# Shared layers of two mixtures read the router's transposed rows; results of the second mixture summed six tiles later, last loads issued ahead of the stores

## The chip, the cores and the metric

The kernel runs on one core of a Trainium2 chip. Its engines work side by side: TensorE (PE; weight loads are listed apart as PEld), VectorE (DVE), ScalarE (ACT), GpSimd (POOL), and SyncE (SP), which here only issues transfers. Each engine takes its own instructions in order and waits on semaphores. The metric is the device time of one execution, in microseconds, of the slowest core; here there is only one. The kernel before took 831.38 us (median of three runs, 828.76 to 834.36).

## The reference

The input x is 16 batches of 128 rows of 256 numbers in 32 bits, with a context of the same shape. Four layers are added to x one after the other, each scaled by tanh of a gate and fed with a layer norm of x:

```python
x = x + tanh(g_xattn[0]) * ssm(ctx, ctx, layernorm(x))        # causal convolution of k (x) v with a kernel, times q
x = x + tanh(g_ffn[0])   * ffn0(layernorm(x))
x = x + tanh(g_xattn[1]) * attention(layernorm(x), ctx, ctx)  # causal, 16 heads of 16
x = x + tanh(g_ffn[1])   * ffn1(layernorm(x))

def ffn0(x):   # 8 experts, 2 for each row, and a shared layer of 1024 hidden
    shared = (silu(x @ sw1.T) * (x @ sw2.T)) @ sw3.T
    top = top_k(sigmoid(x @ router_w.T) + expert_bias, 2)
    return shared + sum(weight(top) * expert(x))               # experts: silu(h1) * h2, 128 hidden

def ffn1(x):   # 32 experts, 6 for each row, and a shared layer of 256 hidden
    shared = square(relu(x @ Ws1.T)) @ Ws2.T
    idx, w = top_6_of_the_4_best_groups(sigmoid(x @ Wr.T + br))
    return shared + sum(w * (square(relu(x @ W1.T)) @ W2.T))   # 128 hidden
```

Each mixture ("ffn") thus uses the same normalised rows twice: for its router and experts, and for its shared layer.

## The kernel before

**Tiles.** A batch b is a tile of 128 rows; `xs[b]` holds it in the on-chip memory throughout. `CHUNKS` cuts the 16 batches into (0-3), (4-7), (8-11), (12-13), (14-15) for the first mixture and attention. `GROUPS` does so for the second mixture, with the last two batches apart.

**Turning rows.** A matrix product needs rows transposed, features on the partitions. `turned` (L197) does it: for each tile one VectorE operation normalises (L211), two TensorE transposes write to PSUM (L214), and one ScalarE copy for two tiles (L216) puts it into a tile `xT` of 128 x 2 x up to 512. In both mixtures this runs twice for each tile. Once for the router: the normalised rows go to `row`, which is also what is sent to the experts, and the transposed ones to `xT_f0{c}` or `xT1_{g}` (names tp_f, lg_r for the router's scores). And once more for the shared layer: rows `xn_s`, transposes `tp_s`, copies `xT_s` (first mixture) and `xTs` (second). `stats` keeps mean and reciprocal deviation (mv, rs) for the second time.

**Stage 1, the convolution,** fills the first 110 us. **Stage 2, the first mixture:** `sends0` (L697) normalises, chooses two experts and scatters each row to its place in a DRAM array `sent0` by indirect transfers from POOL (L725). `shared0` (L639) computes the shared layer of a chunk in 8 blocks: pg, pu (L617), silu and product (hs, L432/433), os (L669). `paced` ties the scatters to hs of the block beside them. `tiles0` takes expert tiles of 128 sorted rows back (got, L756), computes two at a time (xt, gu, eo) and stores them to DRAM; `combine0` gathers a row's two results (L812). **Stage 3, attention,** goes batch by batch (sc L858, ex L875, avT L896), and the rest of the first mixture runs between its steps. Transfers of keys and values (L831, L832) stand on SP.

**Stage 4, the second mixture:** `dispatch` (L951) norms, routes and scatters the rows of a group to `sent`, six places each (L978); `shared1` (L922) does the shared layer: p (L617), relu and square on ACT, o_sh (L625), sum on VectorE (L633). These steps lie beside the last batches of attention. Then `tiles1` (L1164) goes over 114 tiles of 128 expert rows, and further ones if there are more rows. One load (got, L1176) brings six tiles and waits for all scatters to `sent`. Two tiles at a time: copy of weights on ACT (wt, L1187), transposes xt and copy (L1190, L1192), eh (L1197), relu on ACT (er), product on VectorE (ehs, L1207), eo (L1209), copy on ACT (ey, L1218). One scatter per tile by POOL (L1234) writes 128 result rows to their places in the DRAM array `parts`.

**Summing.** A row's six results lie side by side in `parts`. `fetch` (L1137) loads two of six for a batch, once the tiles that can hold its rows are through; it waits for scatters up to five before. `add_fetched` (L1144) adds two products to `xs[b]` (L1148) and, after the third of these, stores the batch (L1150). In the kernel before a fetch is issued at each tile, for the third group of batches two, and is added three tiles later or when over two are held. The last four batches, b12 to b15, are summed after all tiles by `sum_last` (L1152): three loads, six scalings on ACT (L1158), one strided reduction on VectorE (L1160), one addition (L1161), the store.

**Order.** The kernel is written as lists of steps, which `woven` (L1030) interleaves. A scheduler then places the instructions on the engines by its own estimates; on each engine that order is fixed when the kernel is built. `follow` and `after` add a dependency. SP issues all ordinary transfers in one queue, in order; an issue whose wait is not met holds those behind it.

Of the kernel before, what the change touches and what calls it, by code (L numbers as in the profile page):

```python
# [33 lines left out]

E0, SH0, TOPK0 = 8, 8, 2
PARTS0 = [(0, 8), (8, 16)]
NT0 = 8 * TOPK0 + E0 - 1
# [6 lines left out]
GRP = 6  # L44
SURE = 114
FEW = 3
W1_ROW = KC * P + D
# [6 lines left out]
def flamingo(ctx: ExitStack, tc: tile.TileContext, a: dict, out: bass.AP):  # L54
# [163 lines left out]
    def columns(xT, n):  # L218
        return lambda j: xT[:, :, 2 * j * P : min(2 * j + 2, n) * P].rearrange("p c (k t) -> p k c t", t=P)
# [158 lines left out]
    def chunk_T(c, label, scale=1.0, norm=None):  # L378
# [4 lines left out]
        return xT  # L383


    def router(xT, n, rw, ne, label):
# [251 lines left out]

    def shared0(c, norm):  # L639

# [5 lines left out]
        def turn():  # L646
            got["xT"] = chunk_T(c, "s0", norm=norm)

# [46 lines left out]

    norms0 = {}

    def sends0(i):
# [6 lines left out]
        def norm(c):  # L705
            n = CHUNKS[c][1] - CHUNKS[c][0]
            tiles = list(range(*CHUNKS[c]))
            rows = [work.tile([P, ROW], F32, tag="row", name=f"row0_{b}", bufs=8) for b in tiles]
            got.setdefault("rows", []).extend(rows)
            got["xT"] = xT = work.tile([P, KC, TOK], F32, tag="xT", name=f"xT_f0{c}", bufs=4)  # L710
            norms0[c] = stats(tiles, f"f0{c}", keep=True)
            turned(work, tiles, *norms0[c], columns(xT, n), f"f0{c}", keep=lambda k: rows[k][:, :D])

# [207 lines left out]

    def shared1(mv, rs, g):  # L922

# [4 lines left out]
        def turn():  # L928
            got["xT"] = xT = work.tile([P, KC, TOK], F32, tag="xT", name=f"xTs_{g}", bufs=4)
            turned(work, list(range(b0, b1)), mv, rs, columns(xT, b1 - b0), f"s1{g}")  # L930

# [19 lines left out]
    def dispatch(g):  # L951
# [5 lines left out]
        def norm():  # L957
            got["rows"] = rows = [
                work.tile([P, ROW], F32, tag="row", name=f"row{b}", bufs=8) for b in range(b0, b1)
            ]  # L960
            got["xT"] = xT = work.tile([P, KC, TOK], F32, tag="xT", name=f"xT1_{g}", bufs=4)
            tiles = list(range(b0, b1))
            got["norm"] = stats(tiles, f"f1{g}", keep=True)
            turned(work, tiles, *got["norm"], columns(xT, n), f"f1{g}", keep=lambda k: rows[k][:, :D])

# [26 lines left out]
        for t in range(n):  # L992
            sends += [lambda t=t: send(t), *wait[1:]]
        shares[g] = lambda: shared1(*got["norm"], g)
        return [norm, *wait[1:], choose, *wait, place, *sends]
# [44 lines left out]
    def sums0(c):  # L1040
        return [lambda b=b: combine0(b) for b in range(*CHUNKS[c])]

    def with_sums0(c):

        steps = shared0(c, norms0[c])
        for k, add in enumerate(sums0(c)):
            steps[3 + k] = lambda now=steps[3 + k], add=add: (now(), add())
        return steps + [nothing, lambda: begin(c), nothing]
# [3 lines left out]
    for step in sendA[:2]:  # L1052
        step()
    woven(shared0(0, norms0[0]), sendA[2:] + [nothing] * 2)
    more = shared0(1, norms0[1])
    woven(tiles0(0, gotA, scatA, "sc"), [nothing] * 3 + sendB + [nothing] * 6, more[:5])
    woven(sums0(0), more[5:8])
    begin(0)
    beside = [
        lambda: more[8:-1] + [lambda: (more[-1](), [step() for step in sums0(1)])] + tiles0(1, gotB, scatB)  # L1060
        + [lambda: begin(1), nothing],
# [58 lines left out]
    def group(b):  # L1120
        return next(c for c, (b0, b1) in enumerate(GROUPS) if b < b1)
# [11 lines left out]

    todo = [(b, k0) for b in range(GROUPS[FEW][0]) for k0 in range(0, TOPK1, 2)]
    fetched = []

# [6 lines left out]

    def add_fetched():  # L1144

        _, b, k0, part = fetched.pop(0)
        for k in range(2):
            V.scalar_tensor_tensor(xs[b], part[:, k, :], gates[:, b, k0 + k : k0 + k + 1], xs[b], ALU.mult, ALU.add)  # L1148
        if k0 + 2 == TOPK1:
            nc.sync.dma_start(out=out[b], in_=xs[b])  # L1150

    def sum_last(b):  # L1152

        part = work.tile([P, TOPK1, D], F32, tag="big", name=f"part{b}", bufs=BIGS)
        for k0 in range(0, TOPK1, 2):
            load_results(part[:, k0 : k0 + 2], b, k0, len(results))
        for k in range(TOPK1):
            S.activation(part[:, k, :], part[:, k, :], AF.Copy, scale=gates[:, b, k : k + 1])  # L1158
        s = work.tile([P, D], F32, tag="xn", name=f"sum{b}", bufs=3)
        V.tensor_reduce(s, part.rearrange("p k d -> p d k"), AX.X, ALU.add)  # L1160
        V.tensor_tensor(xs[b], xs[b], s, ALU.add)  # L1161
        nc.sync.dma_start(out=out[b], in_=xs[b])

    def tiles1(t0, t1):  # L1164
        for t in range(t0, t1):
# [79 lines left out]

            while fetched and (fetched[0][0] <= t - 3 or len(fetched) > 2):
                add_fetched()
            for _ in range(2 if todo and group(todo[0][0]) + 1 == FEW else 1):
                if todo and t + 1 >= last_tile(group(todo[0][0])) + 6:
                    fetch(t)  # L1250
# [11 lines left out]
    with tc.If(used > SURE * P):  # L1262
        tiles1(SURE, NT1)
    for b in range(GROUPS[FEW][0], B):
        sum_last(b)

# [51 lines left out]
```

## Time and profile before

| what | us |
|---|---|
| runs, median (lowest to highest) | 831.38 (828.76 to 834.36) |
| profiled execution | 832.41, its span 830.6 |
| granted TensorE clock, mean | 0.919 |

The profiled execution is the span and 1.8 us around it. Busy time by stretch, in us of TensorE and VectorE, with the granted clock:

| stretch | what runs | length | PE | DVE | clock |
|---|---|---|---|---|---|
| 110 to 180 | shared layer of chunk 0, routing, scatters | 70 | 62.57 | 36.82 | 0.85 |
| 180 to 250 | first expert tiles, shared layer of chunk 1 | 70 | 67.13 | 33.27 | 0.98 |
| 560 to 633 | routing and shared layer of the second mixture | 73 | 60.00 | 51.79 | 0.91 |
| 633 to 718 | expert tiles of the second mixture | 85 | 76.41 | 40.37 | 0.96 |
| 718 to 802 | the same, with fetched results | 84 | 63.20 | 54.72 | 0.93 |
| 802 to 831 | sums of the last four batches | 29 | 0 | 17.56 | |

A row of the list of groups reads: line, engine, operation, names (buffer numbers left out), shapes, count, then busy us and mean ns of one, and what the engine's idle time ahead of these was ended by. In a timeline or the chain, a line begins with the start and the length in us; a bracket gives idle time ahead and what ended it. The chain is followed back from the end of the execution: at each step to what released the instruction. Some rows of groups that the change touches:

```profile
L1148 DVE SCALAR_TENSOR_TENSOR x<-part,gates,x 128x256 f32<-128x256 f32 x72 | 33.9, 483 | 19.1 <-DMA part<-parts 18.1 <-DVEq L1262 0.5
L211 DVE TENSOR_SCALAR xn_s<-x,mv_f,rs_f 128x256 f32<-128x256 f32 x32 | 12.7, 411 | 1.7 <-PE tp_at L214 0.7 <-PE tp_s L214 0.5 <-PE pos L568 0.3
L214 PE MATMUL tp_s<-ident,xn_s 128*128 128x128 f32 x64 | 12.5, 322 | 2.6 <-DVE xn_s L211 1.0 <-ACT xTs L216 0.7 <-ACT pT L885 0.6
L1160 DVE TENSOR_REDUCE sum<-part 128x256 f32<-128x1536 f32 x4 | 11.0, 2762 | 6.5 <-ACT part L1158 6.5
```

### The profile page before, as it was taken

Reading aid. Unit: us, or ns where it says so; the run is one execution under the profiler, and the core shown is the slowest. Engines: PE = TensorE matmul, PEld = TensorE weight load, DVE = VectorE, ACT = ScalarE, POOL = GpSimd, SP = SyncE. Lnnn points to the kernel's source line nnn. Section 1 sums busy time; section 2 is a strip of 40 time slices with the busy share of each in tenths; the row PEclk is TensorE's granted clock in tenths of the full one; section 3 lists DMA queues with packets and bytes.
Section 4 is the critical chain, followed back from the end, with each engine's and each line's share of the span. In section 5 each row is a group of like instructions: output and inputs, shape, how many; then the busy total and the mean of one; then the engine's idle time right before and its main releaser. Section 6 shows DMA issues by size and latency. Waiting matters only on the chain.

```text
span 830.6 us, 12160 instructions
## 1 busy us (share of the span) xinstructions
PE 703.4 (85%) x3928; PEld 496.4 (60%) x3928; DVE 541.2 (65%) x1579; ACT 367.6 (44%) x811; POOL 332.9 (40%) x326
## 2 busy tenths in 40 slices
PE   6999979989999799999969989958867999788820
PEld 3444445567775577656547747735546898677720
DVE  5999995335446754568667874685883555476756
ACT  2110037115322666652356354426524777566624
POOL 3756702300516100012272057007462677766640
PEclk8999978999999999999979987969987999999975
DMA  8999996122442233541143034063125676788575
GB/s 266 327 371 274 269 262 166 58 72 83 154 131 83 64 102 106 132 116 30 46 124 65 13 89 118 15 164 113 67 100 190 210 228 190 247 291 262 187 244 180
DMA packets 134016, 128.97 MB, mean 155 GB/s; under 512 B 42976, under 2 KB 117888, under 8 KB 133824
## 3 DMA queue, kind: packets, MB, share of 16 engines
q1 hardware_dynamic: 120704, 91.61, 39.5%
q0 software_dynamic: 13152, 36.52, 12.3%
q8 instruction: 32, 0.52, 0.3%
q14 instruction: 32, 0.26, 0.1%
q10 hardware_dynamic: 96, 0.05, 0.0%
HBM read 64.23 MB, written 63.92 MB: 154 GB/s over the span
## 4 chain that ended last, share of the span: by engine, by line
PE 46%; DVE 25%; DMA 10%; issue 7%; ACT 6%; POOL 3%; ACTq 1%; SPq 1%; DVEq 0%; POOLq 0%
PE y L339 7%; DMA part<-parts 4%; PE gu L782 4%; PE eo L1209 3%; PE sc L858 3%; PE pu L617 3%; PE pg L617 3%; PE eh L1197 3%; DVE mn L869 3%; PE eo L792 2%; PE pt L882 2%; PE os L669 2%; ACT ex L875 2%; PE avT L896 2%; PE lg_r L391 2%
## 5 line engine op out<-in xcount | busy, mean ns | idle before, releaser
L978 POOL DMA_INDIRECT sent<-row,dst x96 | 94.0, 979 | 123.8 <-DVE dst L609 94.3
L1234 POOL DMA_INDIRECT parts<-ey,to x114 | 111.6, 979 | 58.9 <-issue 23.2
L875 ACT ACTIVATE ex<-sc,mn 128x128 f32<-128x128 f32 x256 | 71.6, 385 | 68.0 <-DVE mn L869 67.9
L812 POOL DMA_INDIRECT part<-parts,places x32 | 31.2, 975 | 144.6 <-DVE rd L912 88.8
L339 PE MATMUL y<-kv,toe 128*128 128x512 f32 x192 | 85.0, 597 | 0.0
L1209 PE MATMUL eo<-wt,ehs 128*128 128x256 f32 x228 | 62.0, 403 | 17.4 <-DVE ehs L1207 17.3
L331 POOL TENSOR_TENSOR kv<-cT 128x1024 f32<-128x1024 f32 x32 | 60.6, 1893 | 38.0 <-PE y L339 33.2
L725 POOL DMA_INDIRECT sent<-row,places x32 | 31.2, 976 | 103.5 <-DVE places L504 38.2
L1187 ACT COPY wt<-wts 128x512 f32 x114 | 66.3, 620 | 13.9 <-issue 8.6
L617 PE MATMUL pg<-xT_s,wts 128*128 128x512 f32 (+1 forms) x160 | 66.3, 535 | 1.9 <-DVE silu L432 1.9
L1197 PE MATMUL eh<-xts,wt 128*128 128x128 f32 x456 | 64.7, 286 | 2.8 <-ACT wt L1187 2.8
L1197 PEld LDWEIGHTS eh<-xts,wt 128*128 128x128 f32 x456 | 62.2, 201 | 8.2 <-ACT wt L1187 4.1
L617 PE MATMUL pu<-xT_s,wts 128*128 128x512 f32 (+1 forms) x160 | 63.7, 517 | 1.9 <-DVE hs L433 1.9
L669 PE MATMUL os<-wts,hs 128*128 128x256 f32 x256 | 65.0, 387 | 0.0
L339 PEld LDWEIGHTS y<-kv,toe 128*128 128x128 f32 x192 | 36.0, 192 | 41.2 <-issue 29.1
L669 PEld LDWEIGHTS os<-wts,hs 128*128 128x128 f32 x256 | 48.4, 194 | 15.7 <-issue 9.7
L1209 PEld LDWEIGHTS eo<-wt,ehs 128*128 128x128 f32 x228 | 40.9, 197 | 25.2 <-DVE ehs L1207 20.7
L1192 DVE COPY xts<-xt 128x512 f32<-128x512 f32 x57 | 38.7, 686 | 25.5 <-PE xt L1190 18.7
L869 DVE TENSOR_REDUCE mn<-sc 128x4 f32<-128x512 f32 x64 | 41.6, 684 | 20.3 <-PE sc L858 20.0
L782 PEld LDWEIGHTS gu<-xts,wt 128*128 128x128 f32 x368 | 46.4, 196 | 8.6 <-DVE xts L776 4.8
L782 PE MATMUL gu<-xts,wt 128*128 128x128 f32 x368 | 49.2, 283 | 1.9 <-DVE xts L776 1.8
L1218 ACT COPY ey<-eo 128x512 f32<-128x512 f32 x57 | 33.4, 586 | 33.7 <-PE eo L1209 29.3
(250 smaller groups left out, 1360.0 us busy)
## 6 DMA issues: line engine op xcount, KB each, us to landing
sent<-keys SPq DMA_DIRECT2D x1, 17018.0 KB
got<-sent SPq DMA_DIRECT2D x19, 804.0 KB, 5.0
part<-parts SPq DMA_DIRECT2D x48, 256.0 KB, 4.7
sent<-keys SPq DMA_DIRECT2D x2, 2944.0 KB
got<-sent SPq DMA_DIRECT2D x22, 256.0 KB, 3.0
parts<-ey SPq DMA_DIRECT2D x22, 256.0 KB, 2.1
wts<-in_sw SPq DMA_DIRECT2D x3, 1024.0 KB, 11.8
wts<-in_w SPq DMA_DIRECT2D x3, 1024.0 KB
```

Source lines behind the costliest of these rows:

```text
L331: G.tensor_tensor(kv, c[:, :, hs].unsqueeze(3).to_broadcast(full), c[:, :, hs].unsqueeze(2).to_broadcast(full), ALU.mult)
L339: T.matmul(y[:, lb * TOK : (lb + 1) * TOK], lhsT=t[:, off : off + P], rhs=kv[:, kc * HALF : (kc + 1) * HALF].rearrange("p b i j -> p (b i ...
L617: T.matmul(ps, lhsT=w(kc), rhs=xT[:, kc, :n], start=(kc == 0), stop=(kc == KC - 1))
L669: T.matmul(o[:, k * D : (k + 1) * D], lhsT=hs[j][:, t * P : (t + 1) * P], rhs=wC[:, j, :], start=False, stop=(j == SH0 - 1 and k == len(ts ...
L782: T.matmul(gu[:, half * D + u * P : half * D + (u + 1) * P], lhsT=wt[:, u, w : w + P], rhs=xt[:, u * D + kc * P : u * D + (kc + 1) * P], s ...
L869: least = V.tensor_reduce(mn[:, 4 * r : 4 * r + 4], scs[r].rearrange("p (h t) -> p h t", t=P), AX.X, ALU.min)
L875: S.activation(ex[:, i, :], scs[r][:, at : at + P], AF.Exp, bias=mn[:, i : i + 1], scale=-1.0)
L978: ins = G.indirect_dma_start(out=sent[:, :], out_offset=bass.IndirectOffsetOnAxis(ap=dst[:, t, k : k + 1], axis=0), in_=row, in_offset=None,)
L1187: S.copy(wt[:, i], wts[:, bass.ds(offsets[u % GRP], W1_ROW)])
L1197: T.matmul(eh[:, i * P : (i + 1) * P], lhsT=wt[:, i, cols], rhs=xt[:, i * D + kc * P : i * D + (kc + 1) * P], start=(kc == 0), stop=(kc == ...
L1209: T.matmul(eo[:, i * D : (i + 1) * D], lhsT=h[:, i * P : (i + 1) * P], rhs=wt[:, i, KC * P :], start=True, stop=True,)
L1234: ins = G.indirect_dma_start(out=parts[:, :], out_offset=bass.IndirectOffsetOnAxis(ap=to[:, t % GRP : t % GRP + 1], axis=0), in_=y[:, t % ...
```

## The change

It has three parts.

*Shared layers.* They no longer normalise and transpose a second time; they take the router's `xT`. For the first two chunks of the first mixture (`HERE = 2`) this is the tile in the on-chip memory itself. For the others, and for all six groups of the second mixture, `put` writes the tile to a DRAM array and `again` reads it back into a new tile before the shared layer. That is 9 stores and 9 loads on SP, of 128, 256 or 512 KB. One block more of chunk 1's shared layer goes ahead of attention's first queries (`more[5:9]`).

*Summing.* For the first two groups of batches a fetch is issued at every second tile instead of every one, up to three may be held, and each is added six tiles later (`LATE`) instead of three. Each addition has a dependency on the copy of the current pair's transposed rows (`turned_rows`). A finished batch is stored when the next one is finished.

*The end.* All loads of the last four batches are issued first. The stores of the batches finished by then, and of the last four, wait for the last load. The strided reduction is replaced by one addition of 128 x 768 and three of 128 x 256.

```diff
--- before.py
+++ after.py
@@ -33,6 +33,7 @@
 WARM = 22
 
 E0, SH0, TOPK0 = 8, 8, 2
+HERE = 2
 PARTS0 = [(0, 8), (8, 16)]
 NT0 = 8 * TOPK0 + E0 - 1
 W0_ROW = 3 * D
@@ -43,6 +44,7 @@
 GROUPS = [(0, 4), (4, 8), (8, 12), (12, 14), (14, 15), (15, 16)]
 GRP = 6
 SURE = 114
+LATE = 6
 FEW = 3
 W1_ROW = KC * P + D
 W1_END = E1 * W1_ROW
@@ -382,6 +384,17 @@
         turned(work, tiles, mv, rs, columns(xT, len(tiles)), f"{label}{c}", scale=scale)
         return xT
 
+    def put(xT, n, label):
+
+        kept = dram.tile([P, KC, n], F32, tag=f"kept_{label}", name=f"kept_{label}")
+        nc.sync.dma_start(out=kept, in_=xT[:, :, :n])
+        return kept
+
+    def again(kept, n, label):
+        xT = work.tile([P, KC, TOK], F32, tag="xT", name=f"xT_{label}", bufs=4)
+        nc.sync.dma_start(out=xT[:, :, :n], in_=kept)
+        return xT
+
 
     def router(xT, n, rw, ne, label):
 
@@ -636,7 +649,7 @@
 
         return [[(b - b0, b) for b in range(i, min(i + 2, b1))] for i in range(b0, b1, 2)]
 
-    def shared0(c, norm):
+    def shared0(c):
 
         b0, b1 = CHUNKS[c]
         n = (b1 - b0) * P
@@ -644,7 +657,7 @@
         got, hs = {}, [None] * SH0
 
         def turn():
-            got["xT"] = chunk_T(c, "s0", norm=norm)
+            got["xT"] = turned0[c] if c < HERE else again(turned0[c], n, f"s0{c}")
 
         def hidden(j):
             cols = slice(j * P, (j + 1) * P)
@@ -693,7 +706,7 @@
             follow(ins, other, reason)
 
 
-    norms0 = {}
+    turned0 = {}
 
     def sends0(i):
 
@@ -708,8 +721,8 @@
             rows = [work.tile([P, ROW], F32, tag="row", name=f"row0_{b}", bufs=8) for b in tiles]
             got.setdefault("rows", []).extend(rows)
             got["xT"] = xT = work.tile([P, KC, TOK], F32, tag="xT", name=f"xT_f0{c}", bufs=4)
-            norms0[c] = stats(tiles, f"f0{c}", keep=True)
-            turned(work, tiles, *norms0[c], columns(xT, n), f"f0{c}", keep=lambda k: rows[k][:, :D])
+            turned(work, tiles, *stats(tiles, f"f0{c}"), columns(xT, n), f"f0{c}", keep=lambda k: rows[k][:, :D])
+            turned0[c] = xT if c < HERE else put(xT, n * P, f"f0{c}")
 
         def choose(c):
             if c == chunks[0]:
@@ -919,15 +932,14 @@
         return [lambda: scores(0), lambda: scores(1), turn, values, add]
 
 
-    def shared1(mv, rs, g):
+    def shared1(kept, g):
 
         b0, b1 = GROUPS[g]
         n = (b1 - b0) * P
         got, hs = {}, []
 
         def turn():
-            got["xT"] = xT = work.tile([P, KC, TOK], F32, tag="xT", name=f"xTs_{g}", bufs=4)
-            turned(work, list(range(b0, b1)), mv, rs, columns(xT, b1 - b0), f"s1{g}")
+            got["xT"] = again(kept, n, f"s1{g}")
 
         def hidden(j):
             ps = up(lambda kc: ws[:, j, kc * P : (kc + 1) * P], got["xT"], n, f"p1_{g}_{j}")
@@ -960,8 +972,8 @@
             ]
             got["xT"] = xT = work.tile([P, KC, TOK], F32, tag="xT", name=f"xT1_{g}", bufs=4)
             tiles = list(range(b0, b1))
-            got["norm"] = stats(tiles, f"f1{g}", keep=True)
-            turned(work, tiles, *got["norm"], columns(xT, n), f"f1{g}", keep=lambda k: rows[k][:, :D])
+            turned(work, tiles, *stats(tiles, f"f1{g}"), columns(xT, n), f"f1{g}", keep=lambda k: rows[k][:, :D])
+            got["kept"] = put(xT, n * P, f"f1{g}")
 
         def choose():
             got["chosen"] = choose1(got["xT"], g)
@@ -991,7 +1003,7 @@
         sends = []
         for t in range(n):
             sends += [lambda t=t: send(t), *wait[1:]]
-        shares[g] = lambda: shared1(*got["norm"], g)
+        shares[g] = lambda: shared1(got["kept"], g)
         return [norm, *wait[1:], choose, *wait, place, *sends]
 
     aT, begun = {}, {}
@@ -1042,7 +1054,7 @@
 
     def with_sums0(c):
 
-        steps = shared0(c, norms0[c])
+        steps = shared0(c)
         for k, add in enumerate(sums0(c)):
             steps[3 + k] = lambda now=steps[3 + k], add=add: (now(), add())
         return steps + [nothing, lambda: begin(c), nothing]
@@ -1051,13 +1063,13 @@
     sendB, gotB, scatB = sends0(1)
     for step in sendA[:2]:
         step()
-    woven(shared0(0, norms0[0]), sendA[2:] + [nothing] * 2)
-    more = shared0(1, norms0[1])
+    woven(shared0(0), sendA[2:] + [nothing] * 2)
+    more = shared0(1)
     woven(tiles0(0, gotA, scatA, "sc"), [nothing] * 3 + sendB + [nothing] * 6, more[:5])
-    woven(sums0(0), more[5:8])
+    woven(sums0(0), more[5:9])
     begin(0)
     beside = [
-        lambda: more[8:-1] + [lambda: (more[-1](), [step() for step in sums0(1)])] + tiles0(1, gotB, scatB)
+        lambda: more[9:-1] + [lambda: (more[-1](), [step() for step in sums0(1)])] + tiles0(1, gotB, scatB)
         + [lambda: begin(1), nothing],
         lambda: with_sums0(2),
         lambda: with_sums0(3) + [lambda: load_w1(12, W0_END // W1_ROW)],
@@ -1132,7 +1144,10 @@
 
 
     todo = [(b, k0) for b in range(GROUPS[FEW][0]) for k0 in range(0, TOPK1, 2)]
-    fetched = []
+    fetched, done = [], []
+
+    def store(b):
+        return nc.sync.dma_start(out=out[b], in_=xs[b])
 
     def fetch(t):
         b, k0 = todo.pop(0)
@@ -1141,26 +1156,31 @@
         load_results(part, b, k0, min(t - 5, len(results)))
         fetched.append((t, b, k0, part))
 
-    def add_fetched():
+    def add_fetched(behind=None):
 
         _, b, k0, part = fetched.pop(0)
         for k in range(2):
-            V.scalar_tensor_tensor(xs[b], part[:, k, :], gates[:, b, k0 + k : k0 + k + 1], xs[b], ALU.mult, ALU.add)
+            ins = V.scalar_tensor_tensor(
+                xs[b], part[:, k, :], gates[:, b, k0 + k : k0 + k + 1], xs[b], ALU.mult, ALU.add
+            )
+            if behind is not None:
+                follow(ins, behind, "the tiles go first")
         if k0 + 2 == TOPK1:
-            nc.sync.dma_start(out=out[b], in_=xs[b])
-
-    def sum_last(b):
-
+            done.append(b)
+
+    def fetch_last(b):
         part = work.tile([P, TOPK1, D], F32, tag="big", name=f"part{b}", bufs=BIGS)
         for k0 in range(0, TOPK1, 2):
             load_results(part[:, k0 : k0 + 2], b, k0, len(results))
+        return part
+
+    def sum_last(b, part):
+
         for k in range(TOPK1):
             S.activation(part[:, k, :], part[:, k, :], AF.Copy, scale=gates[:, b, k : k + 1])
-        s = work.tile([P, D], F32, tag="xn", name=f"sum{b}", bufs=3)
-        V.tensor_reduce(s, part.rearrange("p k d -> p d k"), AX.X, ALU.add)
-        V.tensor_tensor(xs[b], xs[b], s, ALU.add)
-        nc.sync.dma_start(out=out[b], in_=xs[b])
-
+        V.tensor_tensor(part[:, :3, :], part[:, :3, :], part[:, 3:, :], ALU.add)
+        for k in range(3):
+            V.tensor_tensor(xs[b], xs[b], part[:, k, :], ALU.add)
     def tiles1(t0, t1):
         for t in range(t0, t1):
             if t % GRP == 0:
@@ -1243,9 +1263,12 @@
                 tc.declare_no_dep(ins.ins, load.ins, reason="later tiles have no row of a chunk that is summed")
             results.append(ins)
 
-            while fetched and (fetched[0][0] <= t - 3 or len(fetched) > 2):
-                add_fetched()
-            for _ in range(2 if todo and group(todo[0][0]) + 1 == FEW else 1):
+            slow = todo and group(todo[0][0]) + 1 < FEW
+            while fetched and (fetched[0][0] <= t - LATE or len(fetched) > (3 if slow else 2)):
+                add_fetched(turned_rows)
+            while t1 == SURE and len(done) > 1:
+                store(done.pop(0))
+            for _ in range(t % 2 if slow else 2):
                 if todo and t + 1 >= last_tile(group(todo[0][0])) + 6:
                     fetch(t)
 
@@ -1261,8 +1284,14 @@
     )
     with tc.If(used > SURE * P):
         tiles1(SURE, NT1)
-    for b in range(GROUPS[FEW][0], B):
-        sum_last(b)
+
+    last = range(GROUPS[FEW][0], B)
+    loaded = [fetch_last(b) for b in last]
+    for b in done:
+        follow(store(b), summed[-1], "loads go first")
+    for b, part in zip(last, loaded):
+        sum_last(b, part)
+        follow(store(b), summed[-1], "loads go first")
 
 
 # ---- launch: one core; the host only transposes, pads and regroups ----
```

## The prediction

> **What bounds the kernel now.** First I read the page's busy table, slices and chain of waits:
>
> ```profile
> PE 703.4 (85%) x3928; PEld 496.4 (60%) x3928; DVE 541.2 (65%) x1579; ACT 367.6 (44%) x811; POOL 332.9 (40%) x326
> ...
> PEclk8999978999999999999979987969987999999975
> ...
> PE 46%; DVE 25%; DMA 10%; issue 7%; ACT 6%; POOL 3%; ACTq 1%; SPq 1%; DVEq 0%; POOLq 0%
> ```
>
> TensorE carries the span until about 720 us, yet only 46% of the chain is its own work. I therefore asked for busy time by stage, and for the chain at each stage's end. There are three seams (stage ends) where TensorE is not the limit.
>
> Seam one, 110 to 180 us. TensorE is busy 62.57 of 70 us at a mean clock of 0.85. Its timeline:
>
> ```profile
> 118.38 1.99 PE L391 MATMUL lg_r<-rw,xT_f 128*128 128x8 f32 x16
> 120.22 1.09 PE L214 MATMUL tp_f<-ident,row 128*128 128x128 f32 x8
> 121.55 1.68 PE L214 MATMUL tp_s<-ident,xn_s 128*128 128x128 f32 x8 [0.23 <-ACT xT_f L216]
> 124.04 3.58 PE L391 MATMUL lg_r<-rw,xT_f 128*128 128x8 f32 x16 [0.81 <-ACT xT_s L216]
> 127.47 2.91 PE L617 MATMUL pg<-xT_s,wts 128*128 128x512 f32 x3
> ```
>
> The second turning (tp_s) and the second group's router scores stand ahead of the shared layer. Its first product starts at 127.47. The scatters of this chunk are paced by the shared layer's hs; the last starts at 173.81 and the tile stage's first load at 176.37.
>
> Seam two is the tile stage and what frees it. Here POOL's scatters run at a fixed pace until they stall:
>
> ```profile
> 722.86 0.97 POOL L1234 DMA_INDIRECT parts<-ey,to  x1 [0.30 <-issue]
> 724.13 0.98 POOL L1234 DMA_INDIRECT parts<-ey,to  x1 [0.30 <-issue]
> 727.63 0.96 POOL L1234 DMA_INDIRECT parts<-ey,to  x1 [2.52 <-ACT ey L1218]
> ```
>
> The chain says why: VectorE waited for a load of fetched results, then TensorE ran slowly.
>
> ```profile
> 718.98 4.71 DMA part<-parts
> ...
> 723.79 0.48 DVE x L1148
> 724.27 0.34 DVE ehs L1207
> 724.62 0.04 issue
> 724.66 3.78 PE eo L1209 x8
> ```
>
> Seam three is the end. After the last scatter (802.30) there is no matmul: loads of the last four tiles, then four reductions in a row.
>
> ```profile
> 809.58 5.10 DMA part<-parts
> 814.67 0.03 ACTq L1158
> 814.70 0.44 ACT part L1158 x2
> 815.14 0.02 issue
> 815.16 2.80 DVE sum L1160
> ```
>
> **The sum, part by part**, is made against the profiled execution (832.41 us, span 830.6); the median of the runs, 831.38, is 1.0 lower.
>
> **Shared layer 0, first chunk.** Eight tp_s (1.68 us), two ACT copies (1.07) and four xn_s go. In the changed kernel's order on TensorE, pg_0_0 stands directly after the first half of the second group's turning, where 121 us was, not 127.47. The second router group's matmuls still come between, 2 us at the first group's speed (1.99) against 3.58 now. Two table loads (1.28 us each) leave ACT's stretch. The first block then ends 4 to 5 us sooner, and the hs that pace the scatters with it. From below: nothing, if the routing (s_r at 127.65, first scatter 137.81) becomes the bound; from above the whole 7 us. I take **4.0**, from the nearest row (1.68 + 0.81 + 1.6 of slow router matmuls).
>
> **Second chunk, 180 to 250.** TensorE is busy 67.13 of 70 us, so work removed counts: the chain has 0.76 + 0.45 us of tp_s. **1.2**. Nothing if the puts delay loads: three puts stand among the got loads on SP, each waiting for an ACT copy of xT_f; the shared layer covers these loads.
>
> **250 to 560.** 16 more tp_s of layer 0 and those of the first groups of layer 1, 0.11 us each where TensorE runs full, beside attention; that is some 3 us of TensorE. Against it, three puts stand on SP among keys and values loads, and wait for ACT. The loads are issued well ahead; if that cover goes, each blocked load costs a landing (3.0 us median of a 256 KB load), three times. I take **1.0**, bounds +9 slower to 4 faster.
>
> **Layer 1's shared layer, 560 to 633.** The tile stage's first load goes at 633.43 after POOL's last `sent` scatter (ends 631.82) and TensorE/ACT's shared work (631.3 to 632). Both have to shrink. VectorE is on the chain: the xn_s at 586.46, 589.52, 590.08 and 590.80 (0.32 each) go. On TensorE tp_s and then p (3.59 us at 606.36) now stand ahead of the router's lg_r at 610.02; in the new order the routing of groups 4 and 5 comes before that p, some 4.5 us earlier. POOL waits for b14 and b15 were 1.86 and 2.82. The gain is 4 to 6 on POOL's side, less on TensorE's, which also holds 0.66, 0.44 and 0.89 us of tp_s. I take **3.5**, bounds 7 faster to 6 slower: here four reloads each wait for a put's landing, and the p matmuls wait for them. Cover: group 5's copy is done near 605, a put and a reload take 2.1 + 3.0 us, and its p matmuls run after 620. Queued behind a blocked reload on SP are only the other reloads and the tile stage's first load.
>
> **Tile stage.** An unstalled stream is 646.42 + 114 x 1.275 = 791.8, against 802.30: 10.5 us of stalls, beginning when fetches begin. VectorE's L1148 group waited 18.1 us for loads. From a scatter's start to the next tile's result it takes 1.0 (the scatter), 1.6 (until its load is issued), 2.9 to 4.9 (issue to landing) and some 2.8 (two adds, ehs, eo, ey): 8.3 to 10.3 us. At 1.275 us a scatter, a distance of 7 scatters between the fetched one and the next ehs behind the add leaves 7.95 plus what is queued, 8 leaves 9.2 and 9 leaves 10.5; sevens stall, and eights at times. In VectorE's order of before, of the first 24 fetches two have distance 7 and four 8, and two fetches per pair of tiles (four adds of 0.40) fill VectorE besides: with 1.2 us of the tiles' own work, 2.8 of the 2.55 us that two scatters take. Afterwards one fetch per pair makes it 2.0, and most distances are 9 to 11, but the order that the scheduler makes still has five sevens and one eight. The delay of six tiles is thus half realised. Stalls of 0.4 to 2.2 us at each seven leave 4 to 5 us, 5.0 taken: 10.5 - 5.0 = **5.5**, bounds 1.5 (only the crowding goes) to 9.5.
>
> The clock is part of these stalls: after 4.64 us without a matmul eo x8 took 3.78 us, at a granted clock of 0.65 from 726 to 731, where the next one took 1.89 at 1.00; and after only 2.54 us, at 762.66, it took 2.89, at 0.70. The Trainium skill, "TensorE: Matmul & The Clock Gate", Part 1, says that the clock has a half and a full state alone and drops after at least one idle window of about 3.4 us. The first stall agrees; the second, shorter than that window, lost the clock all the same, so here the row decides. By the rule a remaining stall of 2 us would cost no slow stretch, and five of them would give about 1 us each more than I count: 809 in place of 814.
>
> **End.** The first last-load was issued 5.4 us after the last scatter's end, at 807.69; the end came 22.9 later. Afterwards all loads go first, 14 of 256 KB about 0.45 apart; ACT then scales 24 times 0.406 = 9.7 us from about 5 us on; the last sum is one 128x768 addition (a row of that size took 0.95) and three of 0.34, and the store 2.8. This gives 5 + 9.7 + 2.0 + 2.8 = 19.5, or 21.7 if the loads arrive at 250 GB/s only. Four reductions of 2.8 leave the chain; ACT is late next. Stores of finished tiles now wait for the last load, and ACT's work covers them. Gain **3.4**, bounds 1 to 4.5.
>
> Sum: 4.0 + 1.2 + 1.0 + 3.5 + 5.5 + 3.4 = 18.6, so 832.4 - 18.6 = **814**.
>
> **Rivals.**
> (a) *The late sums do not become late.* The sevens stall as before; each wait is 2 to 3 us and the clock falls again. Then the tile stage gives its lower bound 1.5 or less: 832.4 - (18.6 - 4.0 to 5.5), **818** to 819. For it: the distances. Against: VectorE's load per pair falls from 2.8 to 2.0.
> (b) *The stages are held by the scatter streams,* not by TensorE: the last `sent` scatter is the gate at both routings, and its places come no earlier. The shared layers then give 1 us at each and 5.5 + 3.4 stay: about **822**; together with (a) 827.
> (c) *The round trip through DRAM is the new wait.* Place: SP's queue, in order, at groups 2 to 5 of layer 1 and the puts among attention's loads. A reload waits for a put, the put for ACT, and the next loads for the reload. Price: a put (2.1, the median of the 256 KB stores) and a reload (3.0) with some 0.5 us of issue each, 6 us; at four groups 24, and 6 more for keys. Of the 18.6, 8.7 are then lost with it (4.0 + 1.2 + 3.5 of the shared layers): 832.4 - 9.9 + 30 = 852 with all uncovered, **838** with half. It ends above 832 from the point where the uncovered waits pass 10 us in sum, 2.5 us per reload of these four. For it: SP issues in order, and the chain already counts part loads of 4 to 5 us. Against: DMA is only 27% busy in that stage.
> (d) *The change does little*: removed turnings lay beside other work; all shared-layer parts give nothing, and (a) holds: 832.4 - 3.4 = **829**.
>
> **How the numbers follow.** Forecast 0.47; (a) 0.18; (b) 0.14; (d) 0.09; (c) 0.12. The low end, 803, is the upper bounds of the first chunk (3 more), of layer 1's shared layer (3.5) and of the tile stage (4) together; up to 830 the range takes in (a), (b) and (d); (c) and a little below are left out. About 1% (8.3 us) is what a measurement here can tell from no change. Under 823: forecast, (a) and most of (b), 0.76; within 1%: 0.14; over 839.7: 0.10.
>
> **What would show it.** Right: pg starts near 121; first got of the tile stage of layer 1 at 622 to 625; no eo group above 3 us; POOL's stalls after the first fetch under 6 us; at the end ACT's scaling is continuous and no reduction is seen. Wrong: waits of p1 matmuls for xT_s, or of SP for ACT among the keys, over 2 us; L1148's successor still waiting over 10 us for part loads; a last `sent` scatter that ends no earlier than 631 less the first seams' gain. What would make it wrong is a TensorE order that is held by the reloads, or loads at the end that land much later when 14 are in flight at once.

## The result, and the profile after

The changed kernel takes 826.26 us (median of 20 runs, 822.21 to 829.31), the kernel before 831.23 in the same comparison (826.28 to 834.85). The ratio is 0.9939, with a 95% interval from 0.9924 to 0.9954: 5 us faster, where 18.6 were forecast. The profiled execution took 826.2 us, its span 824.5.

The busy row and the clock row of the page of the changed kernel:

```profile
PE 686.3 (83%) x3864; PEld 483.6 (59%) x3864; DVE 526.4 (64%) x1555; ACT 355.2 (43%) x792; POOL 333.6 (40%) x326
...
PEclk9999979899999799999979999779987999999985
```

TensorE is busy 17 us less (686.3 against 703.4; the removed tp_s were 12.5), and the span is 6.1 us shorter. Where these 6.1 us lie is seen when the span is cut at events that both kernels have. The lengths below, in us, are differences of times in the timelines of TensorE and POOL, one execution for each kernel; the last four columns are experiments, told below (`a_only`, `bc_late`, `late_ehs_2`, `held_late_g1`). One execution can lie some us off its kernel's median: that of `late_ehs_2` took 813.6 us, its median is 816.9.

| from ... to | before | after | shared layers alone | late, old shared layers | late, new shared layers | late and held |
|---|---|---|---|---|---|---|
| start to end of the convolution's matmuls | 106.7 | 105.8 | 106.4 | 106.5 | 106.7 | 106.7 |
| to the first mixture's last scatter | 130.6 | 129.5 | 126.9 | 130.9 | 124.4 | 125.7 |
| to group 2's first scatter (most of attention) | 321.2 | 322.7 | 322.6 | 320.1 | 322.1 | 321.7 |
| to the end of the last scatter to `sent` | 73.3 | 72.9 | 72.9 | 72.2 | 72.9 | 68.7 |
| to the first scatter of results | 14.6 | 14.3 | 14.4 | 13.7 | 14.2 | 14.4 |
| to the last scatter of results (113 steps) | 154.9 | 154.6 | 155.4 | 145.3 | 146.2 | 146.7 |
| to the end | 29.3 | 24.7 | 28.9 | 25.2 | 25.3 | 25.5 |

Of the 6.1 us, 4.6 are the end, and 0.9 lie in the convolution, which the change does not touch. Of the shared layers' three rows the first gains 1.1, attention loses 1.6 and the last gains 0.4. The tile stage, for which 5.5 were forecast, gains 0.3.

*Seam one.* The shared layer starts where the order said. TensorE's timeline of the changed kernel:

```profile
117.52 1.95 PE L404 MATMUL lg_r<-rw,xT_f 128*128 128x8 f32 x16 [0.35 <-ACT xT_f L218]
...
119.80 3.38 PE L630 MATMUL pg<-xT_f,wts 128*128 128x512 f32 x4
```

pg starts at 119.80, not 127.47. Yet POOL's first scatter started at 136.99, not 137.81, and the last of this chunk at 171.75, not 173.81; 0.9 of both is the convolution's earlier end.

*Seam two.* POOL's timeline of the changed kernel, at its first stall:

```profile
721.67 0.97 POOL L1254 DMA_INDIRECT parts<-ey,to  x1 [0.30 <-issue]
722.94 1.21 POOL L1254 DMA_INDIRECT parts<-ey,to  x1 [0.30 <-issue]
727.56 0.97 POOL L1254 DMA_INDIRECT parts<-ey,to  x1 [3.41 <-ACT ey L1238]
```

It stalls at the same place, and for longer: 3.41 us, where it was 2.52. VectorE's timeline tells why (a bracket gives the idle time ahead):

```profile
714.50 0.42 DVE L1227 TENSOR_TENSOR ehs<-er,eh 128x256 f32<-128x256 f32 x1
714.83 1.28 DVE L1212 COPY xts<-xt 128x512 f32<-128x512 f32 x2
...
722.30 0.48 DVE L1163 SCALAR_TENSOR_TENSOR x<-part,gates,x 128x256 f32<-128x256 f32 x1 [5.96 <-DMA part<-parts]
...
723.53 0.68 DVE L1212 COPY xts<-xt 128x512 f32<-128x512 f32 x1
724.13 0.74 DVE L1227 TENSOR_TENSOR ehs<-er,eh 128x256 f32<-128x256 f32 x2
```

The two row copies (xts) at 714.83 belong to pairs that lie ahead of the next product (ehs). The addition waits for such a copy, as the change asks, and so it stands in front of the next two products. VectorE then sits 5.96 us until the loaded results land, and the products come at 724.13, TensorE's eo after them, at the low clock again (3.47 us for eight; the granted clock was 0.57 from 724 to 728). In all, VectorE waited 30.4 us for loaded results at this line, 18.1 before.

*Seam three.* The chain of the changed kernel at its end:

```profile
807.50 4.37 DMA part<-parts
...
812.17 5.28 ACT part L1180 x13
...
819.48 0.97 DVE part L1181
...
821.39 0.42 DVE x L1183
```

The last loads land at 811.87, ACT's scalings follow one another, and the additions after the last scaling take 2.3 us in all. No reduction is left.

### The profile page after: what moved, and what is told of

It is laid out like the page before. It is cut to its first block, busy times and chain, and to the rows that moved or that the text cites. A ratio compares the mean times of both kernels' runs of the same rounds, so it can differ in the third digit from the quotient of the medians.

```text
span 824.5 us, 11999 instructions
## 1 busy us (share of the span) xinstructions
PE 686.3 (83%) x3864; PEld 483.6 (59%) x3864; DVE 526.4 (64%) x1555; ACT 355.2 (43%) x792; POOL 333.6 (40%) x326
## 5 line engine op out<-in xcount | busy, mean ns | idle before, releaser
L825 POOL DMA_INDIRECT part<-parts,places x32 | 31.1, 971 | 142.2 <-DVE rd L925 89.4
L738 POOL DMA_INDIRECT sent<-row,places x32 | 31.2, 974 | 102.4 <-DVE places L517 37.9
L1217 PE MATMUL eh<-xts,wt 128*128 128x128 f32 x456 | 63.0, 281 | 1.4 <-DVE xts L1212 1.3
L1163 DVE SCALAR_TENSOR_TENSOR x<-part,gates,x 128x256 f32<-128x256 f32 x72 | 34.3, 484 | 32.3 <-DMA part<-parts 30.4
L795 PEld LDWEIGHTS gu<-xts,wt 128*128 128x128 f32 x368 | 48.2, 203 | 7.2 <-DVE xts L789 2.4
L444 ACT ACTIVATE silu<-pg 128x512 f32<-128x512 f32 (+1 forms) x40 | 21.1, 527 | 60.4 <-PE pg L630 60.2
```

The costliest lines, as they stand in the source:

```text
L795: T.matmul(gu[:, half * D + u * P : half * D + (u + 1) * P], lhsT=wt[:, u, w : w + P], rhs=xt[:, u * D + kc * P : u * D + (kc + 1) * P], s ...
L1217: T.matmul(eh[:, i * P : (i + 1) * P], lhsT=wt[:, i, cols], rhs=xt[:, i * D + kc * P : i * D + (kc + 1) * P], start=(kc == 0), stop=(kc == ...
```

## The experiments

Ratios are to the kernel before on the same chip, with 95% intervals; "stall" is the time between the first and the last scatter of results less 113 steps of 1.275 us, from one profile (10.8 before, 10.5 after).

**The parts alone.** `a_only` has the new shared layers and the sums and the end of before; `b_only` has the new fetches and sums alone; `c_only` the new end alone; `a_c` is the change without its sums. The edits are the hunks of the diff.

> The shared layers' part alone: turned rows taken from the router, sums and end as in the kernel before. Theory (the stages are gated by POOL's scatter streams and by the order of the routing on VectorE and TensorE, so the tile stage's first load comes only about 1.2 us earlier): 829 to 831, 0.997 to 1.000 of before. Rival (the forecast's terms hold and the gain is lost later, in the tile stage): the first load of the tile stage 8 us earlier, 822 to 824.

> The later sums alone (a fetch per two tiles, six tiles later), the rest as before. Theory (the sevens in VectorE's order stall as before): 829.5 to 832.5, VectorE's wait for part loads not under 18 us, POOL's stalls 9 to 11 us. Rival (the delay works, something else of the change takes it back): 824 to 827, stalls under 6 us.

> The end alone: last loads ahead of stores, additions in place of the strided reduction. Theory (the end is the change's gain, its tail went from 28.3 to 23.7 us behind the last scatter): 826 to 828. Rival (the tail is shorter only because stores were held back by the new sums): 829 to 831.

> The change without its later sums: shared layers and end new, fetches and additions as before. Theory (later sums are worth nothing): 825 to 827, as the whole change. Rival (they are worth the forecast's 5.5): 830 to 832.

| kernel | median us | ratio (interval) | stall | last scatter to end |
|---|---|---|---|---|
| a_only | 830.42 | 1.0006 (0.9982 to 1.0031) | 11.3 | 28.9 |
| b_only | 830.36 | 0.9998 (0.9975 to 1.0020) | 16.3 | 27.4 |
| c_only | 829.05 | 0.9983 (0.9959 to 1.0008) | 14.7 | 26.8 |
| a_c | 828.56 | 0.9960 (0.9930 to 0.9989) | 12.4 | 26.2 |

The shared layers alone are worth nothing that can be measured, and so are the sums alone; with these the stall is even 16.3 us, above the 9 to 11 that were expected. The end alone saves 2.5 us of its own stretch, and its median is 1.4 lower; that interval holds no change too, and the median lies above the 826 to 828 that were expected, at the edge of the rival's 829 to 831. `a_c` falls between its theory and its rival, and its interval overlaps that of the whole change. The stall changes by 4 us between kernels whose tile stage is written the same (10.8, 11.3, 12.4, 14.7): it is not a fixed cost. That each wait sets off the next is a reading of this, not shown.

**Behind the product.** In the changed kernel each addition is made to wait for the product of the current pair, which in VectorE's order comes two pairs later than the row copy.

```diff
-                V.tensor_tensor(h, r, eh[:, : m * P], ALU.mult)
+                product = V.tensor_tensor(h, r, eh[:, : m * P], ALU.mult)
...
-                add_fetched(turned_rows)
+                add_fetched(product)
```

> The changed kernel (826), where each addition of fetched results waits for the product (ehs) of the current pair instead of its transposed rows. In VectorE's order an addition then stands 10 to 15 scatters behind the scatter it needs, instead of 7 to 11. Theory (the rows' copy runs two pairs ahead of ehs, so the additions were late in name only): POOL's stalls from 10.5 to under 5 us, 820 to 823. Rival (the stalls come from transfers or crowding, not from the place of the additions): stalls 9 to 12 us, 825 to 828.

This and the three runs beside it (`no_sums`, `route_held`, `layer0_only`) went to another chip, where the kernel before took 944 us; 0.9864 (0.9817 to 0.9910) there says little, so it was run again:

> The changed kernel with additions behind the product (ehs) of the current pair, again, on a chip where the kernel before takes 830 (in the first try all kernels, the one before too, took 13% longer). Theory: stalls of POOL's scatters from 10.5 to under 6 us, 820 to 823. Rival: 825 to 828.

816.9 us, ratio 0.9848 (0.9818 to 0.9877), where the changed kernel has 0.9939: by the ratios 7 to 8 us less, for one changed dependency, and more than was expected. The stall is 2.1 us, not 10.5. POOL at the two scatters between which the changed kernel stalled, VectorE beside them, and the wait of the additions in the list of groups:

```profile
718.02 0.96 POOL L1254 DMA_INDIRECT parts<-ey,to  x1 [0.30 <-issue]
719.29 0.97 POOL L1254 DMA_INDIRECT parts<-ey,to  x1 [0.30 <-issue]
```

```profile
717.70 0.41 DVE L1227 TENSOR_TENSOR ehs<-er,eh 128x256 f32<-128x256 f32 x1
...
718.78 0.47 DVE L1163 SCALAR_TENSOR_TENSOR x<-part,gates,x 128x256 f32<-128x256 f32 x1
719.17 0.41 DVE L1227 TENSOR_TENSOR ehs<-er,eh 128x256 f32<-128x256 f32 x1
```

```profile
L1163 DVE SCALAR_TENSOR_TENSOR x<-part,gates,x 128x256 f32<-128x256 f32 x72 | 34.2, 482 | 18.1 <-DMA part<-parts 16.4 <-DVEq L1285 0.8
```

The first addition now finds its load landed. VectorE still waits 16.4 us for loads at this line, nearly as long as before the change, but behind products that are out already; what the waits cost is decided by what stands behind them.

The same one edit in the kernel before (three tiles later, a fetch at each tile):

> The kernel before with one edit: its additions of fetched results (three tiles later, a fetch at each tile) wait for the product (ehs) of the current pair. In VectorE's order they stand 10 to 14 scatters behind the scatter they need, instead of 7 to 12. Theory (the place behind ehs is what counts, not the six tiles and not the halved rate of fetches): 0.988 to 0.992. Rival (the rate of fetches crowds VectorE too): 0.995 to 1.000, stalls of 7 to 11 us.

824.96 us, ratio 0.9947 (0.9930 to 0.9965), stall 7.5. That is the rival's side, with its stall. The place of the additions is worth some 4 us by itself. The halved rate of fetches and the six tiles together bring the rest (the stall goes from 7.5 to 1.3 in `bc_late`, below), but only with additions behind the product: without that they were worth nothing (`b_only`). No run tells these two apart.

**The price of all sums.** The fetches and additions of the first twelve batches are left out.

```diff
-    todo = [(b, k0) for b in range(GROUPS[FEW][0]) for k0 in range(0, TOPK1, 2)]
-    fetched, done = [], []
+    todo = []
+    fetched, done = [], list(range(GROUPS[FEW][0]))
...
-            while t1 == SURE and len(done) > 1:
-                store(done.pop(0))
```

> The changed kernel without the fetches and additions of the first twelve batches (their mixture sum is left out; the last four are summed). It prices all that the sums cost the tile stage. Theory (all of the stalls come from the sums): 145 us between first and last scatter instead of 154.6, 814 to 818. Rival (scatters, weights' copies or memory traffic stall by themselves): 820 or more.

> The changed kernel without fetches and additions of the first twelve batches (that part of the sum is left out), again on a chip where the kernel before takes 830. Theory: 144 to 146 us between first and last scatter, the floor at one scatter per 1.275 us, 814 to 818. Rival (stalls not from the sums): 820 or more.

On the other chip 0.9866 (0.9802 to 0.9929); on a usual one 815.53 us, 0.9841 (0.9802 to 0.9879), and 143.9 us between first and last scatter, the floor of 113 x 1.275 = 144.1. All of the stall came from the sums, and additions behind the product cost 1.4 us more than none at all (816.9 against 815.5, within the intervals).

**The shared layers where nothing stalls.** `bc_late` has the new sums (behind the product) and the new end, and the shared layers of before.

> The kernel before with the changed sums and end, additions behind ehs, but the shared layers turning their rows themselves. It prices the shared layers' part where the tile stage no longer blurs it: the same with the new shared layers took 0.985 of the kernel before. Theory (reading the router's rows is worth 0 to 2 us): 0.985 to 0.988. Rival (it is worth the forecast's 9.7 and was lost in the tile stage's stalls alone): 0.995 to 0.998.

815.8 us, ratio 0.9844 (0.9825 to 0.9864), against 0.9848 with the new shared layers. Reading the router's rows is worth nothing here either, within the some 3 us that the two intervals leave; the rival, that its gain was lost in the tile stage, falls.

**Where its gain goes.** The mask of group 5 starts at 614.07, not 619.23, 5.2 us earlier; its places are written at 623.13, not 624.04, only 0.9 earlier. TensorE and POOL of the changed kernel:

```profile
614.02 2.86 PE L638 MATMUL o_sh<-ws,h 128*128 128x256 f32 x12
616.72 0.18 PE L577 MATMUL pos<-mb,before_me 128*128 128x32 bf16 x1
```

```profile
617.57 0.97 POOL L990 DMA_INDIRECT sent<-row,dst  x1 [0.30 <-issue]
623.58 0.97 POOL L990 DMA_INDIRECT sent<-row,dst  x1 [5.04 <-DVE own L1114]
```

The mask is out at 614.25. The matmul on it (pos) starts at 616.72, behind twelve matmuls of the shared layer, and VectorE does seven of the shared layer's sums between 615.6 and 623.1, amid the steps from mask to places. The twelve matmuls stood at the same place before the change (613.98), and the first four sums ahead of the mask; the other three sums came behind the places then, from 628 on. So the mask came earlier, but ran into shared work that had not moved or that had moved forward with it. POOL waits 5.04 us (2.82 before). `route_held` puts these matmuls and sums behind the routing. The routing is written first, and in `down` the matmuls are ordered behind group 5's last pos (`held[0]`), the sums behind its places (`held[1]`):

```diff
-        some(1), at(15, 4), send3[0], choose4, norm5, some(3), send3[1], place4, send4, choose5, some(4), place5, send5,
+        some(1), at(15, 4), send3[0], choose4, norm5, some(3), send3[1], place4, send4, choose5, place5, send5, some(4),
...
+                if held:
+                    queue(ins, held[0])
...
+            if held:
+                queue(ins, held[1])
```

> The changed kernel, where the last group's routing is written ahead of the shared layers' remaining steps, and their second matmuls and additions are ordered behind its positions and places. Theory (the shared steps, ready earlier without their turning, were scheduled in front of the last routing and took 4 us of it): mask to places of group 5 from 9.1 to 5 us, the tile stage's first scatter 3.5 to 4.5 us earlier, 821 to 823. Rival (the stage is bound by TensorE's shared work or by the scatters' own count): 825 to 827.

> The changed kernel with the last group's routing ahead of the shared layers' remaining steps, again on a chip where the kernel before takes 830. Theory: mask to places of group 5 about 5 us instead of 9.1 (5.2 instead of 8.1 in the first try), first scatter of results 3 to 4 us earlier, 822 to 824. Rival (given back in the tile stage): 825 to 828.

```profile
613.72 0.18 PE L577 MATMUL pos<-mb,before_me 128*128 128x32 bf16 x1
...
613.80 3.70 PE L642 MATMUL o_sh<-ws,h 128*128 128x256 f32 x16
```

```profile
618.11 0.97 POOL L998 DMA_INDIRECT sent<-row,dst  x1 [1.44 <-DVE dst L622]
```

The order did what was meant: from mask to places 5.5 us, not 9.1 (4.8 before the change; 5.2 against 8.2 on the other chip), and POOL's wait is 1.44. From b14's first scatter to b15's it is 8.8 us, not 12.4. But the time, 826.33 us, 0.9959 (0.9935 to 0.9983), is no better than the changed kernel's. Where the saving went is not shown: the profile is of an execution of 821.88 us, 4.4 below the median, and its tile stage stalled 10.9 us, much as the changed kernel's (10.5). On the other chip it was 0.9845 (0.9797 to 0.9893). The theory was right on the step and wrong on the time.

`layer0_only` has the second mixture's shared layers as before:

> The changed kernel with the second mixture's shared layers as before; the first mixture's still take the router's rows. Theory (both halves of the first part are worth next to nothing): 825 to 829. It tells whether the 2.4 us that attention takes longer, and the 2.2 us before the last group's scatters, come from the first mixture's half or from the second's.

0.9887 (0.9827 to 0.9947), on the other chip only. There group 5 took 4.8 us from mask to places, against 8.2 with the new shared layers in both mixtures. So this loss comes from the second mixture's half. Whose the longer attention is, it does not tell, since attention itself took 40 to 49 us longer on that chip.

**In attention** the traces show where the removed turning went. POOL issues the 24 scatters of group 1 and then, in the same row, the gathers (L825) of the first mixture's results that VectorE adds to x. POOL and VectorE of the changed kernel, and TensorE just behind; the last line is VectorE of the kernel before:

```profile
513.72 0.97 POOL L990 DMA_INDIRECT sent<-row,dst  x1 [0.30 <-issue]
515.00 0.98 POOL L825 DMA_INDIRECT part<-parts,places  x1 [0.30 <-issue]
```

```profile
517.76 0.48 DVE L832 SCALAR_TENSOR_TENSOR x<-part,gates,x 128x256 f32<-128x256 f32 x1 [12.14 <-DMA part<-parts,places]
```

```profile
520.27 2.08 PE L630 MATMUL pg<-xT_s,wts 128*128 128x256 f32 x4 [10.86 <-DVE silu L445]
```

```profile
518.08 0.48 DVE L819 SCALAR_TENSOR_TENSOR x<-part,gates,x 128x256 f32<-128x256 f32 x1 [1.64 <-DMA part<-parts,places]
```

VectorE and TensorE are done with their own work sooner and wait for the same gathers: VectorE 12.14 us, not 1.64, and TensorE 10.86, not 1.14. From group 1's first scatter to group 2's it is 73.6 us, 73.8 before. What moving the gathers ahead of the scatters would bring was not tried.

**All together.** `held_late` has both edits. `held_late_g1` also orders the sums of the first mixture's shared layer of b12 and b13 behind the places of group 1, since from mask to places of that group the changed kernel takes 12.9 us, not 10.4.

```diff
+                    if c == 3 and 1 in sent_dst:
+                        queue(ins, sent_dst[1])
```

> Both edits together, and a third: the sums of the first mixture's shared layer of b12 and b13 on VectorE are ordered behind the places of group 1's rows. Theory (three places where work that became free early was put ahead of a chain that sets the end): mask to places of group 1 from 12.9 to about 10.5 us, all gains add: 816 to 819. Rival (the tile stage or the scatters' count takes them back): 822 to 826.

> The changed kernel with additions behind ehs and the last group's routing held in front, without the third edit (sums of b12 and b13 behind the places of group 1). Theory (the third edit gave nothing: from the second routing's end to group 2's places 321.3 us with it and 321.6 without): as with it, 0.979 to 0.983. Rival: 0.984 to 0.986.

811.69 us, 0.9802 (0.9764 to 0.9839), and 816.31 us, 0.9833 (0.9799 to 0.9867). Both beat the kernel before and the changed one clearly; between them, and against the late sums alone (0.9848), the intervals overlap. From b14's first scatter on, holding saves 3.6 us in both profiles. The third edit shortened group 1's step to 11.7 us, but from the first mixture's last scatter to group 2's places it still is 321.3 us, against 321.6 with the late sums alone and 320.7 before: this profile shows no gain from it.

## Why the prediction was wrong

The forecast was 814 us in a range of 803 to 830; the kernel took 826. The time is near the one that the text gives to rivals (a) and (b) together, 827. The mechanism of (a), sums that do not become late, is shown by `late_ehs_2`. Of (b), the traces show POOL's row of scatters as the pace in attention, but at the last group the shared layer's own steps as what held the places. That the time fits within 1 us is partly luck: the shared layers brought nothing, where (b) has 2 us, and the end 4.6, where it has 3.4.

**Tile stage, 5.5 forecast, 0.3 found.** The failed step is the sum of 8.3 to 10.3 us from a scatter to the next tile's result, and in it the 2.8 us for "two adds, ehs, eo, ey". For the first stalled group, scatter to landing was sized well: 715.3 (the scatter's start) to 722.28, 7.0 us. From the landing to the next scatter (727.56) it took 5.3, as the steps of other pairs (mine, to, xts) stand between the additions and the products, and eo ran at the low clock. The prediction's own lines of the kernel before already held 3.9 there (723.69 to 727.63). 7.0 + 5.3 = 12.3 us is 9.6 scatters: a distance of 9 is not safe, and by VectorE's order in the trace the changed kernel has four sevens and eleven nines among its first 24 fetches. That the scheduler's order takes half of the six tiles had been seen, but it was priced at 5 us of the 10.5 and cost all of them. The sign of being wrong that the text named, over 10 us of VectorE's waits for loads at this line, came with 30.4. The distances of 13 in `late_ehs_2` (21 of these 24) left 2.1 us.

**Shared layers, 9.7 forecast, none found** (`a_only`, and `bc_late` against `late_ehs_2`). In the first chunk the start was right (119.80 for "near 121"). The lower bound, that the routing becomes the limit, holds for the first scatter: counted from the convolution's end it came 31.2 us later, 31.1 before. The last is 1.1 earlier in this profile by that count, and from 2.1 later to 6.4 earlier in those of the seven other kernels with the new shared layers on chips of the usual speed. So a gain is there in some executions, and it is lost behind. Attention, where I had a gain of 1.0, took 320.9 to 324.5 us in these eight profiles, and 319.5 to 321.2 in the five with the old shared layers. The step that failed there is the price of tp_s "where TensorE runs full": around the first mixture's last gathers POOL's row sets the pace, and TensorE idled 10.86 us. Group 1's step from mask to places took 2.6 longer; the edit that took 1.2 of it back did not bring the time back, so the cause of the longer attention stays open. In the second mixture the forecast had "the routing of groups 4 and 5 comes before that p", and it does, by 5 us at the mask. The step that failed here is that the routing stays in front: twelve of the shared layer's matmuls stood ahead of group 5's positions all the same, and three of its sums, freed from their turning, came ahead of its places, so that the places came only 0.9 earlier.

**The end, 3.4 forecast, 4.6 found,** 2.5 of it by the end's own edit. The rest comes with the new sums (1.9 us in `b_only`); how is not shown, since twelve additions are left after the last scatter in `b_only` as in the kernel before.

**The round trip (rival c) did not show.** What ended TensorE's idle time ahead of matmuls that read the reloaded rows, in the view of tile xT_s of the changed kernel (us, times):

```profile
  DVE silu L445: 23.6, 5
  issue: 14.7, 52
```

No transfer is among them; of the 23.6 us behind silu (5.1 before), 10.86 are the wait for the gathers told above. SP's queue did stand 63.7 us behind the six puts of the second mixture, 25.4 at the longest, in the view of SP's waits (and 4.5 behind the three of the first), and TensorE's weight loads waited 1.1 us for keys in all: the loads behind the puts were far ahead of their use. The 2.5 us per reload from which this rival would have decided the time were not reached.

## What to carry to other kernels

A wait that is meant to make work late should name an instruction by its place in the engine's finished order, not by the tile it belongs to: here the "current" tile's row copy ran two pairs ahead of the product that mattered, and one changed name was worth 7 to 8 us. When work loses an input that it had to wait for, look at what it will be scheduled in front of: an early filler can push back the chain that it was to free. Look too at what the engines wait for next: here the time that the turning left free went into a wait for gathers that stood behind 24 scatters. Where stalls differ by 4 us between kernels with the same stage, price them by leaving their cause out, as was done with the sums here, before forecasting what a smaller delay brings.

## What was not expected of the hardware

TensorE's clock at one place differs between executions of nearly the same order and decides some 3 us. Rows for 110 to 122 us, with TensorE's granted clock (the sixth figure behind the length, ahead of the DMA share and GB/s), of `late_ehs_2` and of `a_c`, whose orders are the same until the tile stage:

```profile
110.00:122.00 12.00, 10.36 (x49) 6.99 (x50) 10.74 (x42) 3.89 (x7) 0.00 (x0) 0.72 1.08 268
```

```profile
110.00:122.00 12.00, 10.97 (x44) 8.36 (x44) 9.23 (x36) 3.01 (x6) 0.00 (x0) 0.50 1.12 263
```

At 0.72 the 16 router matmuls took 2.05 us and the first scatter came at 136.25; at 0.50 they took 3.58 and it came at 139.33. `held_late` (0.50) and `held_late_g1` (0.72) differ in the same way, 139.43 against 136.22. The six times of `held_late` lie at 811.6 to 813.3 and at 819.3 to 820.8, and its profile is of the longest; whether this stretch alone parts them is not shown. The Trainium skill, "TensorE: Matmul & The Clock Gate", Part 1, says that the window by which the clock is set runs free of the kernel, so that the place where the clock rises moves with it; the rows agree in kind, and the shift here is of microseconds, since a whole group of matmuls falls on either side. The new order of the shared layers starts in this stretch; the first mixture's last scatter came at 231.15 in the profile of `late_ehs_2` and at 238.19 in that of `a_c`, 237.32 before.

On one chip every kernel took 13 to 14% longer, the one before too (944 us). There the first 60 scatters of results of the changed kernels took 95 to 99 us, where they take 76.4 on the other. The cause was not looked for.
